# A graph layer on one core: one load of x for two projections, clears and placement steps spread over the first stage, edges loaded four slots ahead

## The chip, the cores and the metric

The kernel runs on one core of a Trainium2 chip. The time is device microseconds of that core for one execution. Five engines run their own instruction streams side by side: PE (matrix multiply), DVE (vector), ACT (scalar and copies), POOL (here: it issues the scatters) and SP (here: it only issues DMAs). Sixteen DMA engines move the data for all of them. An engine takes its instructions strictly in the order in which the program lists them, so an instruction that waits holds back everything behind it on its engine. That holds for SP too: a DMA that waits for a free buffer holds back the DMAs behind it.

## The reference

There are 6,250 nodes with 128 features, and 100,000 edges sorted by `dst`.

```python
row, col = (edge_index[0], edge_index[1])
msg_in = jnp.concatenate([x[row], x[col], edge_attr], axis=-1)
h = msg_in @ W + b
mu = jnp.mean(h, axis=-1, keepdims=True)
var = jnp.mean(jnp.square(h - mu), axis=-1, keepdims=True)
h = (h - mu) * jax.lax.rsqrt(var + LN_EPS) * gamma + beta
msg = jax.nn.relu(h)
out = jax.ops.segment_sum(msg, row, num_segments=x.shape[0])
...
x = _layernorm(x + _L0_gnn_ref(x, edge_index, edge_attr_128, W, b, gamma, beta), axis=-1)
```

`W` has three blocks of 128 rows: for the source node, the target node and the edge. So `h` is a sum of three projections, of `x[src]`, of `x[dst]` and of the edge features.

## The kernel before

**Tiles, slots, stages.** Edges are cut into 782 tiles of 128. Four tiles are a *piece*, and the main loop handles one piece in each *slot* `q`, from 0 to 195. The tiles are divided into five stages (`SPLITS`, L37): slots 0 to 40 are stage 0, then 42 slots, 42, 41 and 30.

**What a slot does.** `edge_loads` (L460) loads the edge features `eT` and the targets' positions `db`, for `DG` = 3 pieces at a time, in two buffers. `edge_window` (L478) loads a window of 42 rows of the projected targets from a table in memory (`xb_d`), in three bf16 parts whose sum has nearly float precision; the table is one of three (`TABLES`), chosen by the slot (`TABLE_FROM`). `edge_hot` (L490, DVE) turns `db` into a one-hot matrix `ohd`, two slots ahead of its use. `edges` (L503, PE) multiplies edge features by `W` (L512) and adds the window's rows through the one-hot (L516). `scatters` (L520) copies the result from PSUM to `hs` (ACT, L524 and L525) and scatters its 128 rows for each tile to a place in `sorted_d` (POOL, L529, four indirect DMAs a slot). `hs` has eight buffers, so the slots may run ahead of the scatters by eight.

**Places.** `places` (L356) works out where each edge's row goes, for a group of 12, 24 or some 42 tiles. It is a generator of eleven steps on DVE and PE: a one-hot over blocks (L368), a running count (L372), counts over partitions (PE, L384 and L385), the offsets (L391, L394), a sum on PE (L409), the place (L413 to L426). Its steps are dealt to slots by hand (`at_slots`, L805 to L810). The *first*, *second* and *third* places are the groups of 12, 24 and 43 tiles at the start of stage 0. `source_blocks` (L228) prepares the block numbers of a range of tiles on DVE.

**Projections in stage 0.** `project(g, k)` (L308) projects four blocks of 128 nodes. With `k` = 1 it makes the target tables: it multiplies `x` by the second block of `W`, splits the result into three bf16 parts on ACT and DVE (L331 to L339) and writes them to the tables (SP, L345). With `k` = 0 it makes `xa`, the sources' projection, which stays in SBUF. Each of the two has its own array of `x` in memory (`xN` in node order, `xT` in block order), loaded by `load_x` (SP, L107) in three buffers. One projection starts in three slots of four and goes on by one step in each slot after.

**Clears.** Before a stage's rows are scattered, the part of `sorted_d` that may stay empty is filled with a marker: `clear_pairs` (L861) issues one DMA (L192) for each of the 25 pairs of blocks of a stage.

**Second half of each stage.** From five slots into the next stage on, `load_pair` (L572, SP, L576) reads the sorted rows of two blocks back (`hl`), and the class `Pair` adds the sources' part, normalizes, applies the relu and sums by node. `work(n)` deals these steps to the slots. The last stage's pairs follow after the last slot, with the final layer norm (`Finish`).

**The order.** PE, DVE, ACT and SP run in the order in which the program lists their work; nothing is reordered. In each slot of stage 0 the list is: projections' next steps, edge loads, the window, clears of the next stage, `edge_hot`, `edges`, `scatters`, places' steps, a new projection with its load of `x`, clears of stage 0, and what `others` names for this slot.

Of the kernel before, what the change touches and what calls it, by code (L numbers as in the profile page):

```python
# [8 lines left out]
F32 = mybir.dt.float32  # L9
# [6 lines left out]
P = 128  # L16
# [10 lines left out]
PT = 4  # L27
WN = 42

TABLES = [(0, 512), (0, 1536), (1024, 6656)]  # L30
PIECES = 196
TABLE_FROM = [0, 13, 40, PIECES]
HALF = PIECES // 2
BANKS = {"hp": 2, "sel": 3, "tr": 1}

# [29 lines left out]
def dram_ap(t, offset, ap):  # L65
    return bass.AP(tensor=t.tensor, offset=t.offset + offset, ap=ap)
# [16 lines left out]
def fast_path(ctx, tc, io, bad_d):  # L83
# [22 lines left out]

    def load_x(g, k):  # L107
        xT = proj_pool.tile([P, XG * P], F32, name="xT", bufs=3)
        n = min(XG * P, (NPAD if k == 0 else TABLES[-1][1]) - g * XG * P)
# [193 lines left out]

    xa = tabs.tile([P, NB, 3 * D], BF16, name="xa")
    acc = tabs.tile([P, NB, ACW], F32, name="acc")
    n_proj = [-(-NB // XG), TABLES[-1][1] // (XG * P)]

    def project(g, k):  # L308

        t0 = g * XG
        m = min(XG, NB - t0) if k == 0 else XG
        xT = xT_of.pop((g, k))
        name = ("sel", "sel", "tr", "sel")[g % 4]
        ps = psum.tile([P, XG, P], F32, name=name, bufs=BANKS[name])
        for j in range(m):
            nc.tensor.matmul(ps[:, j, :], xT[:, j * P:(j + 1) * P], w[:, k, :],
                             start=True, stop=True)
        yield  # L320
        full = ps[:, :m, :]
        if k == 0:
            o = [xa[:, t0:t0 + m, i * D:(i + 1) * D] for i in range(3)]
            full_t = proj_pool.tile([P, XG, D], F32, name="full", bufs=2)
            full = full_t[:, :m, :]
            nc.vector.tensor_tensor(full, ps[:, :m, :], row_bc(bias, m), op=ALU.add)
            yield
        else:
            xb_t = proj_pool.tile([P, 3, XG, D], BF16, name="xb", bufs=4)
            o = [xb_t[:, i, :, :] for i in range(3)]  # L330
        nc.scalar.copy(o[0], full)  # L331
        yield
        rest_t = proj_pool.tile([P, XG, D], F32, name="rest", bufs=2)
        rest = rest_t[:, :m, :]
        nc.vector.tensor_tensor(rest, full, o[0], op=ALU.subtract)
        yield
        nc.scalar.copy(o[1], rest)
        yield
        nc.vector.tensor_tensor(o[2], rest, o[1], op=ALU.subtract)  # L339
        yield  # L340
        if k == 1:
            n0 = g * XG * P
            for (lo, hi), t in zip(TABLES, xb_d):
                if lo <= n0 < hi:
                    nc.sync.dma_start(  # L345
                        dram_ap(t, (n0 - lo) * D, [[XG * D, P], [(hi - lo) * D, 3], [1, XG * D]]),
                        xb_t.rearrange("p i t d -> p i (t d)"))
        yield


# [100 lines left out]
        nc.vector.tensor_copy(bad_d, bad_n)  # L451


    HS, DG = 8, 3
    hs_all = [const.tile([P, PT, ROW], F32, name=f"hs{i}") for i in range(HS)]
    for h in hs_all:
        nc.gpsimd.memset(h[:, :, D:ROW], 0.0)
# [2 lines left out]
    def edge_loads(q, queue=None):  # L460

        if q % DG or q >= PIECES:
            return
        t0 = q * PT
        g = min(DG, PIECES - q)
        eT = edge.tile([P, DG * PT * P], F32, name="eT", bufs=2)
        db = edge.tile([P, DG * PT * P], BF16, name="db", bufs=2)
        for n in ([(0, g)] if q else [(i, 1) for i in range(g)]):
            c0, c1 = n[0] * PT * P, min((n[0] + n[1]) * PT * P, (TILES - t0) * P)
            nc.sync.dma_start(eT[:, c0:c1], io["eT"][:, t0 * P + c0:t0 * P + c1])  # L470
            c1 = (n[0] + n[1]) * PT * P
# [272 lines left out]
    def run(g, n=1):  # L744
        for _ in range(n):
            next(g, None)
# [114 lines left out]
    def clear_pairs(s, n):  # L861
        for p0 in range(cleared[s], min(cleared[s] + n, NB // 2)):
# [3 lines left out]
                tc.add_to_no_dep_group("clear", i.ins)  # L866
            cleared[s] = p0 + 1

    for s, (n_tiles, _, _, _) in enumerate(SPLITS):
        p0, p1 = first_tile[s] // PT, -(-first_tile[s + 1] // PT)  # L870
        slots = p1 - p0
        for i in range(slots):
            q = p0 + i
            for g in groups:
                run(g)
            edge_loads(q + 3)
            edge_window(q + 3)
            if s + 1 < n_split and i >= slots - 30:
                clear_pairs(s + 1, 1 if slots > NB // 2 else 2)
            edge_hot(q + 2)  # L880
            edges(s, q)
            n = steps_due(q + 1) - n_steps
            work(min(n, 1))
            scatters(s, q)
            for g in steps_at.pop(q, []):
                run(g)
            work(n - 1)
            if s == 0:
                if todo and q % 4 != 3:
                    groups = groups[-5:] + [project(*todo.pop(0))]  # L890
                    run(groups[-1])
                    if loads:
                        load_x(*loads.pop(0))
                if 2 <= i:
                    clear_pairs(0, 2)
            if q in others:
                others.pop(q)()
        if s == 0:
            assert not todo and late
# [302 lines left out]
```

## Time and profile before

| | us |
|---|---|
| median of three runs | 1479.99 |
| lowest and highest run | 1478.99, 1490.42 |
| own time of the profiled execution | 1186.86 |
| its span, first to last instruction | 1184.9 |
| PE busy (mean granted clock 0.917 of full) | 969.5 (82%) |
| DVE busy | 926.8 (78%) |
| POOL busy | 837.2 (71%) |
| ACT busy | 623.4 (53%) |
| bytes moved, mean rate | 247.79 MB, 209 GB/s |

The profile is of one execution, and that execution took 293 us less than the median of the runs. Its parts are read against its own time. "Busy" leaves out the time in which an engine waits, and also the time in which it only issues: POOL's scatters count 0.97 us each, and some 0.3 us between two of them is not counted. A line of the timeline gives the start, the duration, the engine, the line of the program, the operation, and in brackets the idle time before it with what ended that. A line of the table of waits gives who waited for whom, the total, how many times, and the longest.

### The profile page before, as it was taken

The page shows a single profiled execution, that of the slowest core. Times are in us where ns is not written, and L with a number is a line of the kernel's source. Part 1 is how long each engine was busy: PE and PEld are TensorE (multiplying, and loading weights), DVE is VectorE, ACT ScalarE, POOL GpSimd, SP SyncE. Part 2 cuts the span into 40 slices and gives each one's busy share as a digit, 9 for nine tenths or more (in the row PEclk, how much of TensorE's full clock was granted, in tenths as well). Part 3 has the DMA queues.
Part 4 walks back from the last instruction along what each step waited for, and adds up shares of the span by engine and source line. Part 5 has one row for each costly group of instructions (what it writes and reads, how often), then busy time and mean ns, then how long its engine had stood idle before and what let it go on. Part 6 is the DMA issues. An engine that isn't in the chain of part 4 may idle for free.

```text
span 1184.9 us, 27181 instructions
## 1 busy us (share of the span) xinstructions
PE 969.5 (82%) x9050; PEld 849.0 (72%) x9050; DVE 926.8 (78%) x2504; ACT 623.4 (53%) x2848; POOL 837.2 (71%) x899
## 2 busy tenths in 40 slices
PE   3565576656889899798989979999898999999994
PEld 2554466545778787687877868788787889877883
DVE  8765288716698997779889778987888788888996
ACT  1222233113465465455556455546555677768996
POOL 2575677777777777777777777777777777743664
PEclk9786687766999999899999989999999999999998
DMA  6499787538587864677877657786766576534551
GB/s 199 151 287 277 233 272 232 182 101 295 170 264 245 262 205 161 221 239 238 264 230 224 193 190 217 250 263 209 227 214 202 183 230 222 170 124 133 161 168 58
DMA packets 113948, 247.79 MB, mean 209 GB/s; under 512 B 45691, under 2 KB 59020, under 8 KB 113798
## 3 DMA queue, kind: packets, MB, share of 16 engines
q1 hardware_dynamic: 87668, 191.99, 52.6%
q0 software_dynamic: 25152, 53.18, 12.7%
q8 instruction: 73, 1.20, 0.4%
q10 hardware_dynamic: 978, 0.80, 0.2%
q14 instruction: 77, 0.63, 0.2%
HBM read 158.36 MB, written 87.52 MB: 208 GB/s over the span
## 4 chain that ended last, share of the span: by engine, by line
DMA 24%; PE 23%; POOL 18%; DVE 14%; issue 10%; ACT 9%; SPq 2%; ACTq 0%; POOLq 0%; DVEq 0%
POOL sorted L529 18%; DMA sorted<-hs,place_i 18%; PE pa L669 6%; DMA db<-drel_d 4%; PE sel L628 4%; PE hp L512 4%; PE beside L409 3%; ACT sq L645 3%; DVE msg L660 3%; PE sel L624 3%; DVE ohe L597 2%; DVE sc L372 2%; ACT ohn L613 2%; ACT fsq L715 2%; PE tr L609 2%
## 5 line engine op out<-in xcount | busy, mean ns | idle before, releaser
L529 POOL DMA_INDIRECT sorted<-hs,place_i x782 | 769.9, 985 | 265.5 <-issue 195.8
L524 ACT COPY hs<-hp 128x512 f32<-128x512 f32 x196 | 114.2, 583 | 390.9 <-DMA sorted<-hs,place_i 234.4
L512 PE MATMUL hp<-w,eT 128*128 128x128 f32 x1564 | 237.8, 300 | 35.1 <-ACT hs L524 26.6
L669 PE MATMUL pa<-msg,ohe 128*128 128x130 f32 x1900 | 246.8, 283 | 13.0 <-DVE acc L677 5.5
L660 DVE SCALAR_TENSOR_TENSOR msg<-sel,rstd,cut 128x128 f32<-128x128 f32 x875 | 247.2, 345 | 9.4 <-PE tr L609 0.5
L628 PEld LDWEIGHTS <-ohn 128*128 128x128 bf16 x2850 | 178.3, 99 | 94.8 <-issue 71.5
L645 ACT ACTIVATE sq<-sel 128x128 f32<-128x128 f32 x875 | 230.4, 282 | 18.1 <-PE sel L628 12.8
L512 PEld LDWEIGHTS hp<-w,eT 128*128 128x128 f32 x1564 | 211.7, 210 | 38.4 <-ACT hs L524 29.0
L669 PEld LDWEIGHTS pa<-msg,ohe 128*128 128x128 f32 x1900 | 228.3, 195 | 15.2 <-issue 8.1
L628 PE MATMUL sel<-xa,ohn 128*128 128x128 bf16 x2625 | 183.6, 222 | 14.8 <-ACT ohn L613 14.0
L645 ACT ACTIVATION_READ_ACCUMULATOR sq<-sel 128x1 f32 x875 | 186.1, 213 | 0.0
L597 DVE TENSOR_TENSOR ohe<-hl,beside 128x1024 f32<-128x1024 f32 (+1 forms) x125 | 144.3, 1156 | 45.8 <-DMA hl<-sorted 19.1
L500 DVE TENSOR_SCALAR ohd<-db,part_w 128x512 bf16<-128x512 bf16 x194 | 71.5, 369 | 93.9 <-DMA db<-drel_d 77.9
L624 PE MATMUL sel<-hl,ident 128*128 128x512 f32 (+1 forms) x250 | 130.6, 605 | 14.2 <-DVE msg L660 14.0
L613 ACT COPY ohn<-tr 128x1024 bf16<-128x1024 bf16 (+1 forms) x125 | 120.6, 965 | 18.3 <-PE tr L609 18.1
L609 PE MATMUL tr<-ident_h,ohe 128*128 128x128 bf16 x950 | 76.2, 224 | 19.7 <-DVE ohe L597 19.7
L516 PE MATMUL hp<-win,ohd 126*128 126x128 bf16 x782 | 81.1, 229 | 9.6 <-DVE ohd L500 5.5
L638 DVE TENSOR_TENSOR sel<-sel,hl 128x512 f32<-128x512 f32 x100 | 69.1, 691 | 12.8 <-PE sel L628 12.8
L648 ACT ACTIVATE std<-ss,eps 128x4 f32<-128x4 f32 (+1 forms) x250 | 74.3, 297 | 8.1
L609 PEld LDWEIGHTS <-ohe 128*128 128x128 bf16 x950 | 60.0, 100 | 22.0 <-DVE ohe L597 21.8
L409 PE MATMUL beside<-far,ident 128*128 128x294 f32 (+10 forms) x304 | 75.3, 402 | 0.0
L516 PEld LDWEIGHTS <-ohd 126*128 126x128 bf16 x782 | 64.5, 103 | 14.3 <-DVE ohd L500 9.0
(156 smaller groups left out, 967.3 us busy)
## 6 DMA issues: line engine op xcount, KB each, us to landing
hl<-sorted SPq DMA_DIRECT2D x100, 528.0 KB
eT<-in_eT SPq DMA_DIRECT2D x64, 768.0 KB
sorted<-empty SPq DMA_DIRECT2D x125, 198.0 KB
db<-drel_d SPq DMA_DIRECT2D x64, 384.0 KB
sorted<-hs,place_i POOLq DMA_INDIRECT x782
hl<-sorted SPq DMA_DIRECT2D x25, 396.0 KB
win<-xb_d SPq DMA_DIRECT2D x196, 31.5 KB
xb_d<-xb SPq DMA_DIRECT2D x15, 384.0 KB
```

The costliest lines, as they stand in the source:

```text
L512: nc.tensor.matmul(hp[:, j, :], eT[:, at], w[:, 2, :], start=j == 0, stop=False, skip_group_check=True)
L516: nc.tensor.matmul(hp[:, j, :], oh[:3 * WN, at], win[:3 * WN, :], start=False, stop=j == m - 1, skip_group_check=True)
L524: evict = nc.scalar.copy(hs[:, :m, 0:D], hp[:, :m, :])
L529: i = nc.gpsimd.indirect_dma_start(out=sorted_d[s][:, :], out_offset=bass.IndirectOffsetOnAxis(ap=place_i[:parts, t:t + 1], axis=0), in_=h ...
L597: nc.vector.tensor_tensor(self.ohe[:, :k, :], self.hl[:, :k, D:D + 1].to_broadcast([P, k, P]), row_bc(iota_p, k), op=ALU.is_equal)
L609: nc.tensor.transpose(tr[:, j, :], half[:, j0 + j, 1::2], ident_h)
L613: nc.scalar.copy(self.ohn[:, :self.k, :], self.tr[:, :self.k, :])
L624: nc.tensor.matmul(sel[:, :m, :], ident, rows, start=True, stop=False)
L628: nc.tensor.matmul(sel[:, j, :], self.ohn[:, j0 + j, :], xa[:, b, i * D:(i + 1) * D], start=not on_pe and i == 0, stop=(j == m - 1 and i = ...
L645: nc.scalar.activation(sq[:, j, :], self.sel[g][:, j, :], AF.Square, accum_out=ss[:, j:j + 1])
L660: nc.vector.scalar_tensor_tensor(self.msg[:, j0 + j, 0:D], self.sel[g][:, j, :], rstd[:, j:j + 1], cut, op0=ALU.mult, op1=ALU.max)
L669: nc.tensor.matmul(self.pa[:, h, :], self.ohe[:, j, :], self.msg[:, j, :], start=(j == h), stop=(j == k - 2 + h))
```

## The change

- **Tables.** The third table covers all 6,400 padded nodes in block order instead of nodes 1,024 to 6,656 in node order, and is used from piece 45 instead of 40. It is written by a new kind of projection, `k` = 2, which reads the same loaded `x` (`xT`) as `k` = 0, right before it. `k` = 1 remains for the first three groups. So 3 loads of `xN` and 13 of `xT` remain of 13 and 13, and 29 projections are made instead of 26. The list of projections alternates `k` = 2 and `k` = 0; a load of `xT` is issued when every second projection starts.
- **Edges.** `DG` is 2 instead of 3, with three buffers instead of two. Loads and windows are issued for slot `q + 4` instead of `q + 3`, after a start of four slots. Pieces 2 and 3 are loaded with piece 0 before the loop.
- **Clears.** Stage 0's clears go from two in each slot from slot 2 on to two and one in turn from slot 1 on. Stage 1's begin 26 slots before the end of stage 0 instead of 30.
- **Places and other steps.** The third places' eleven steps go from slots 3 to 7 to slots 2 to 8. `source_blocks` moves from slots 4 and 8 to 8 and 12, the weights of `k` = 0 and the biases from 6 and 7 to 2 and 3, `open_late` from 40 to 44.

```diff
-TABLES = [(0, 512), (0, 1536), (1024, 6656)]
+TABLES = [(0, 512), (0, 1536), (0, NPAD)]
-TABLE_FROM = [0, 13, 40, PIECES]
+TABLE_FROM = [0, 13, 45, PIECES]
...
-        m = min(XG, NB - t0) if k == 0 else XG
-        xT = xT_of.pop((g, k))
-        name = ("sel", "sel", "tr", "sel")[g % 4]
+        m = XG if k == 1 else min(XG, NB - t0)
+        xT = xT_of[g, k % 2]
+        name = ("sel", "sel", "tr", "sel")[n_banks % 4]
+        n_banks += 1
...
-            nc.tensor.matmul(ps[:, j, :], xT[:, j * P:(j + 1) * P], w[:, k, :],
+            nc.tensor.matmul(ps[:, j, :], xT[:, j * P:(j + 1) * P], w[:, min(k, 1), :],
...
+        if k == 2:
+            nc.sync.dma_start(
+                dram_ap(xb_d[2], t0 * D, [[NB * D, P], [NPAD * D, 3], [1, m * D]]),
+                xb_t[:, :, :m, :].rearrange("p i t d -> p i (t d)"))
...
-    HS, DG = 8, 3
+    HS, DG = 8, 2
...
-        eT = edge.tile([P, DG * PT * P], F32, name="eT", bufs=2)
-        db = edge.tile([P, DG * PT * P], BF16, name="db", bufs=2)
+        eT = edge.tile([P, DG * PT * P], F32, name="eT", bufs=3)
+        db = edge.tile([P, DG * PT * P], BF16, name="db", bufs=3)
...
-            (nc.sync if q else nc.gpsimd).dma_start(
+            (nc.sync if q > 2 else nc.gpsimd).dma_start(
...
     edge_loads(0)
+    edge_loads(2)
     run(first)
...
-    load_x(3, 1)
+    load_x(0, 0)
...
-    todo = [(g, 1) for g in range(1, n_proj[1])] + [(g, 0) for g in range(n_proj[0])]
-    loads = todo[3:]
+    todo = [(g, 1) for g in range(1, n_proj[1])]
+    todo += [(g, k) for g in range(n_proj[0]) for k in (2, 0)]
+    loads = {2 * g + n_proj[1] - 4: (g, 0) for g in range(1, n_proj[0])}
+    n_todo = len(todo)
     others = {1: lambda: bases(range(1, len(TABLES))),
-              4: lambda: source_blocks(8 * n0, TILES // 2),
-              8: lambda: source_blocks(TILES // 2, TILES),
-              6: lambda: weights(0, 1), 7: biases, 10: check_early, 36: check_windows,
-              37: check_bases, 38: cuts, 40: lambda: open_late()}
+              8: lambda: source_blocks(8 * n0, TILES // 2),
+              12: lambda: source_blocks(TILES // 2, TILES),
+              2: lambda: weights(0, 1), 3: biases, 10: check_early, 36: check_windows,
+              37: check_bases, 38: cuts, 44: lambda: open_late()}
...
-            at_slots = [3, 3, 4, 4, 4, 4, 5, 5, 6, 7, 7]
+            at_slots = [2, 2, 3, 3, 3, 5, 5, 6, 6, 7, 8]
...
-            edge_loads(q + 3)
-            edge_window(q + 3)
-            if s + 1 < n_split and i >= slots - 30:
+
+            while ahead <= min(q + 4, 3 + q + q // 3):
+                edge_loads(ahead)
+                edge_window(ahead)
+                ahead += 1
+            if s + 1 < n_split and i >= slots - (30 if s else 26):
...
-                    if loads:
-                        load_x(*loads.pop(0))
-                if 2 <= i:
-                    clear_pairs(0, 2)
+                    if n_todo - len(todo) in loads:
+                        load_x(*loads.pop(n_todo - len(todo)))
+                clear_pairs(0, 1 + i % 2 if 1 <= i else 0)
```

More of the change, by code (lines that the diff above doesn't have):

```diff
@@ L108, in load_x @@
         xT = proj_pool.tile([P, XG * P], F32, name="xT", bufs=3)
-        n = min(XG * P, (NPAD if k == 0 else TABLES[-1][1]) - g * XG * P)
+        n = min(XG * P, (NPAD, TABLES[1][1])[k] - g * XG * P)
         nc.sync.dma_start(xT[:, :n], io[("xT", "xN")[k]][:, g * XG * P:g * XG * P + n])
@@ L305, in fast_path @@
     acc = tabs.tile([P, NB, ACW], F32, name="acc")
-    n_proj = [-(-NB // XG), TABLES[-1][1] // (XG * P)]
+    n_proj = [-(-NB // XG), TABLES[1][1] // (XG * P)]
+    n_banks = 0
     def project(g, k):
+        nonlocal n_banks
         t0 = g * XG
-        m = min(XG, NB - t0) if k == 0 else XG
-        xT = xT_of.pop((g, k))
-        name = ("sel", "sel", "tr", "sel")[g % 4]
+        m = XG if k == 1 else min(XG, NB - t0)
+        xT = xT_of[g, k % 2]
+        name = ("sel", "sel", "tr", "sel")[n_banks % 4]
+        n_banks += 1
         ps = psum.tile([P, XG, P], F32, name=name, bufs=BANKS[name])
         for j in range(m):
-            nc.tensor.matmul(ps[:, j, :], xT[:, j * P:(j + 1) * P], w[:, k, :],
+            nc.tensor.matmul(ps[:, j, :], xT[:, j * P:(j + 1) * P], w[:, min(k, 1), :],
                              start=True, stop=True)
@@ L329, in project @@
             xb_t = proj_pool.tile([P, 3, XG, D], BF16, name="xb", bufs=4)
-            o = [xb_t[:, i, :, :] for i in range(3)]
+            o = [xb_t[:, i, :m, :] for i in range(3)]
         nc.scalar.copy(o[0], full)
@@ L342, in project @@
             n0 = g * XG * P
-            for (lo, hi), t in zip(TABLES, xb_d):
+            for (lo, hi), t in zip(TABLES[:2], xb_d):
                 if lo <= n0 < hi:
@@ L867, in clear_pairs @@
             cleared[s] = p0 + 1
+    ahead = 3
     for s, (n_tiles, _, _, _) in enumerate(SPLITS):
@@ L898, in fast_path @@
         if s == 0:
-            assert not todo and late
+            assert not todo and not loads
     work(4 * len(pairs) + LEAD + 18 - n_steps)
@@ L1178 @@
     xT = xp.reshape(P, NB, D).transpose(2, 1, 0).reshape(D, NB * P)
-    n_all = TABLES[-1][1]
+    n_all = TABLES[1][1]
     xN = np.zeros((n_all, D), x.dtype)
-    xN[:N] = x
+    xN[:] = x[:n_all]
     xN = xN.reshape(n_all // (XG * P), P, XG, D).transpose(3, 0, 2, 1).reshape(D, n_all)
```

## The prediction

> **What bounds the kernel now.** I read the page first, for the engine that repeats. Its first column of the second block below is the group, then busy time and mean ns of one, then the idle time just before them and what ended most of it.
>
> ```profile
> span 1184.9 us, 27181 instructions
> POOL 2575677777777777777777777777777777743664
> DMA  6499787538587864677877657786766576534551
> L529 POOL DMA_INDIRECT sorted<-hs,place_i x782 | 769.9, 985 | 265.5 <-issue 195.8
> L500 DVE TENSOR_SCALAR ohd<-db,part_w 128x512 bf16<-128x512 bf16 x194 | 71.5, 369 | 93.9 <-DMA db<-drel_d 77.9
> ```
>
> POOL stands at 7 tenths from the fifth slice to the thirty-fifth and never moves: that is a metronome, not an engine with slack. The timeline of POOL shows its beat: a scatter takes 0.97 us, and the next follows 0.30 us later, whatever is ready. It is broken in one stretch only:
>
> ```profile
> 49.30 0.97 POOL L529 DMA_INDIRECT sorted<-hs,place_i  x1 [0.31 <-issue]
> 58.58 0.97 POOL L529 DMA_INDIRECT sorted<-hs,place_i  x1 [8.31 <-ACT hs L525]
> ...
> 94.97 0.97 POOL L529 DMA_INDIRECT sorted<-hs,place_i  x1 [3.89 <-ACT hs L525]
> ...
> 133.26 0.96 POOL L529 DMA_INDIRECT sorted<-hs,place_i  x1 [0.31 <-issue]
> 140.45 0.97 POOL L529 DMA_INDIRECT sorted<-hs,place_i  x1 [6.23 <-ACT hs L525]
> ```
>
> The sum: first scatter at 23.9, 782 x 1.27 = 993, gaps for hs, long scatters (782 x (985 - 967 median) = 14), last one ended at 1053.9, then 131.0 of last-stage pairs and output. 23.9 + 993 + 23.4 + 14 + 131 = 1185, the span; the execution's own time is 1186.86. What is the 23.4? The table of waits, taken for 23 to 142 us alone (total, times, longest):
>
> ```profile
> ACT xb L331 <- DMA xb_d<-xb: 37.5, 7, 11.6
> DVE ohd L500 <- DMA db<-drel_d: 33.4, 5, 9.6
> PE beside L384 <- DVE cnt L381: 27.0, 3, 13.8
> POOL sorted L529 <- ACT hs L525: 23.4, 6, 8.3
> ```
>
> POOL's six waits for hs are 23.4 us (27.4 in the whole span). The chain of waits for the first 170 us (start, us, what) names what stands behind the first of them, and the stretches of 30 us (DMA share and GB/s last) why it was late:
>
> ```profile
> 40.02 7.95 DMA db<-drel_d
> 48.06 0.35 DVE ohd L500
> 48.41 2.31 DVE sc L372
> 50.75 2.45 DVE sc L372
> ...
> 60.00:90.00 30.00, 18.22 (x122) 15.44 (x121) 18.06 (x45) 7.53 (x18) 22.16 (x22) 0.85 0.94 292
> 90.00:120.00 30.00, 15.62 (x97) 14.76 (x97) 15.98 (x27) 8.52 (x21) 17.98 (x19) 0.61 0.91 274
> ```
>
> DVE stands in order: while it waits for db at 48, the 43-tile places step behind it waits, PE waits for its counts (13.8 us at 53.7), behind that the edge matmuls, then hs, then POOL. DMA is full: per slot a first-stage program moves 256 KB eT, 128 db, 31.5 win, 264 scatter, 2 clears x 198, 3/4 x 256 xT, 3/4 x 384 xb: 1,555 KB, which at the mean of the two rows' last column, 283 GB/s, is 5.6 us, over the 5.08 of four scatters.
>
> At the other end the chain reads:
>
> ```profile
> 831.21 7.02 DMA sorted<-hs,place_i
> 838.37 0.59 ACT hs L524
> ```
>
> From there to the end it runs over PE, DVE and ACT, but it hangs on a scatter through the hs buffers (8 slots), so a POOL that is earlier moves all of it.
>
> **The change part by part.** *One load of x, two projections.* 10 of 13 xN loads go (10 x 256 KB = 2.6 MB), 13 xT loads stay. Table 2 is written in 13 pieces (12.5 x 384 KB) instead of 11: +0.6 MB. Net -2.0 MB, 7 us of DMA time at 283 GB/s. Projections go from 26 to 29: each added one is eight rows of PE (1.1 us when warm, 2.05 cold), two ACT copies (0.59 + 0.62) and two DVE subtracts (0.69 + 0.68): +3.3 PE, +3.6 ACT, +4.1 DVE us, spread to slot 36 where POOL's lead covers them (DVE is 4.8 us busy of 30 at 240 to 270). They end four slots later, and table 2 is first read at slot 41, two slots after its last write (entry 26 of the list starts in slot 34, its write is five slots on): 10 us, against the 1.1 to 11.6 us that ACT waited for such writes; if it is late, up to 8 slots x 5.08 us of POOL's filled hs stand before it. Nothing charged. The xT load now takes a buffer freed one projection before, so SP no longer stands at L110 for the matmul just issued (22.4 + 9.0 us between 23 and 260, with db and win loads queued behind).
>
> *Clears spread.* 1.5 a slot instead of 2, stage 1's from slot 15, not 11. No bytes go. Per slot now: 256 + 128 + 31.5 + 264 + 297 + 96 (xT) + 144 (xb) = 1,217 KB, 4.4 us at 283 GB/s, under the beat. In slots 15 to 17 both clears meet: 2.5 x 198, 1,415 KB, 5.1 us: even, for three slots. The last clear is issued at slot 17; scatters from slot 19 wait for it. A landing of 8 us (like db's) fits in two slots; without that cover, one wait of 8 us at most.
>
> *Third places spread.* Same instructions; PE's count matmul comes two slots after DVE's cnt instead of in the same slot, so edge matmuls no longer stand behind it. DVE's need in slots 2 to 8: places 13.6 (oh 2.45, scans 4.8, cnt and at 1.1, far 2.5, product 1.3, rest 1.5), source blocks 3.8 (53.6 to 57.4), weights and biases 1.6, ohd 7 x 0.35, 5.5 projections x 1.7: 31 us of 35.6. It fits, narrowly. What can remain is between 0 and 9.9 (the two gaps there, 8.3 and 1.6, unchanged); the near row is the 1.55 us at 70 us, where DVE was full and not waiting. I take 4 with the even slots 15 to 17.
>
> *Edges two pieces at a time, four slots ahead.* 98 loads of eT and db instead of 65: 66 more DMAs on SP at a median of 0.36 and 0.42 us, 26 us of a queue whose five longest waits sum to 509. db is asked for at slot q for ohd of slot q + 2, not q + 1: 10 us against landings of 7 to 9. That takes most of DVE's 77.9 us; after 142 POOL never starved, so there it is worth nothing but perhaps 1 us at the end (db wait at 1002 us in the chain; POOL's last landing is only some 5 us ahead of the final pairs' start). At the start, 256 KB more of eT go ahead of the first windows: 1.2 us at the 226 GB/s of 20 to 30 us, of which 0.3 is covered (the first hs was done at 23.59, the scatter began at 23.88): +1. The bounds are 0, as eT of piece 0 still goes first, and 1.2.
>
> Here a rule speaks against the change. The trace has db landings of 7.95 and 8.87 us for 384 KB behind 768. The Trainium skill ("DMA: Bandwidth & Descriptors", Measured under Bandwidth, and the fit in Anatomy of one DMA) wants 1 MiB a transfer, and gives a fixed 2.0 us to each. By it 66 more transfers are 132 us of transfer latency, and if POOL stood behind each, the kernel would be 113 us slower. The same trace has 16 engines 0.94 busy with five kinds of transfer overlapped, so the fixed part runs beside other transfers: I take 0, and the rule's fit was made on another queue kind.
>
> Sum: 23.4 - 4 residual - 1 start + 1 end = 19.4 us off 1186.86: 1167.5.
>
> **The runs shown** lie 293 us above that execution (1478.99 to 1490.42), and the profile doesn't say where. If it is POOL's beat (293/782 = 0.37 us a scatter), a slot is 6.6 us, the 5.6 us of DMA fit before the change too, and perhaps 8 us are left to gain. If it is DMA (247.79 MB in 1480 is 167 GB/s), 2.0 MB are 12 us, and the gaps are larger than seen. If it is PE or lies outside, all 19.4 stay. I carry the difference over as it is: 1479.99 - 19.4 = 1460.6.
>
> **The rivals.** *Hidden* (0.28): the beat of the runs is slower or DVE's 31 of 35.6 us don't fit; 0 to 14 us gained, 1466 to 1480. For it: the 293 us. Against: gaps of 6.2 us at 140 are DMA's, not DVE's.
> *Slower* (0.16): SP in its order. An edge load waits for the matmuls of the slot before (L470, 82.4 us in 38 waits, 2.2 each); 33 more such holds are 72 us, and pair loads (L576) stand behind them. From 840 us PE and DVE have no slack, so a hold that makes hl late is paid. hl is asked for six steps ahead, 1.5 slots at the last stretch's four steps a slot; it decides when holds eat those 8 us. A quarter of 72 exposed is 18 us, nearly cancelling the gain; half is 36: 1480 + 36 - 19 = 1497. Against: DVE waited for hl four times, 19.1 us in all.
> *Not done* : if db is asked for earlier but SP still stands at L110 or L470, the first gap stays and 10 us are gained: inside the second case.
>
> **How the numbers follow.** Gaps closed: 0.56, own range 1447 (all 23.4 and 3 at the end, by 1.25) to 1465. A measurement of this kernel tells about 1%, 14.8 us. Faster by more than that (under 1465.2) 0.56, within 0.29, slower 0.15. The range reaches 1440 (DMA-short runs with larger gaps) to 1486, leaving out 2 in 10, mostly of the slower case.
>
> **What would show it.** POOL's waits for hs before 142 us near 4, not 23.4; last scatter ends near 1035; DVE's waits for db under 25 us; DMA share at 60 to 120 below 0.9; SP's waits at L110 nearly gone. Wrong if POOL shows new gaps at slots 17 to 19 or 41, if hl waits grow after 840, or if POOL closes its gaps and the runs don't follow.

## The result: 0.3% faster where 1.3% was forecast

| | before | after |
|---|---|---|
| median of 20 runs each, us | 1472.69 | 1469.45 |
| lowest to highest, us | 1464.44 to 1490.42 | 1464.94 to 1486.12 |

The ratio is 0.9972, with a 95% interval of 0.9949 to 0.9995: some 3 to 4 us of 1473 where 19.4 were forecast. The time lies in the range of the prediction, which was 46 us wide, and the direction is right, but the gain is about a sixth to a fifth of what the sum gave. Even that is small beside what lies between sessions: the medians of the kernel before in three later ones of the same kind are 1478 to 1490 us.

One thing has to be known to read the rest: the runs of this kernel fall in two conditions, of 1167 to 1192 us and of 1461 to 1507 us for the kernels before and after, and in each of the five sessions of the experiments (each on another chip) all runs were in the same one. They are called A and B here. The profile that the prediction was worked out from was an execution in A; the runs it was to predict were in B, and so is the profile of the changed kernel. On which chips those were taken is not on record.

The page of the changed kernel first: its span, PE's and POOL's tenths in 40 slices, the shares of the chain that ended last, and the two groups that answer to those shown of before.

```profile
span 1468.7 us, 27422 instructions
PE   4736455446877878786868778787877998888995
POOL 3667666665555555555655555555555554550565
PE 55%; issue 16%; DVE 12%; another core or an unknown queue 8%; ACT 7%; DMA 1%; SPq 1%; ACTq 0%; DVEq 0%
L536 POOL DMA_INDIRECT sorted<-hs,place_i x782 | 770.9, 986 | 532.3 <-ACT hs L532 310.6
L507 DVE TENSOR_SCALAR ohd<-db,part_w 128x512 bf16<-128x512 bf16 x194 | 69.5, 359 | 66.4 <-remote 53.1
```

POOL's scatters take what they took before (986 ns against 985), but POOL's row of sevens has become a row of fives, while PE's stands at 7 to 9 in the second half: the beat of 1.27 us is gone. Before, the scatters' idle time was mostly their own issue time (195.8 of 265.5 us); now 310.6 of 532.3 us are waits for `hs`. POOL is starved all along and has no share in the chain, which runs over PE and over time in which an engine waits for nothing that the trace names ("issue"). The table of waits of the same execution (total, times, longest) has both:

```profile
POOL sorted L536 <- ACT hs L532: 310.6, 110, 6.7
...
PE sel L635 <- issue: 71.2, 104, 2.3
...
PE hp L519 <- issue: 67.5, 46, 12.9
...
PE tr L616 <- issue: 46.6, 62, 1.4
```

Summed over all of PE's lines, these gaps without a releaser (over 0.15 us each) are 260.5 us, in 307 gaps. In the profile of before there are none. PE's timeline from 611 to 616 us shows what they look like (start, duration, line, count, and in brackets the gap):

```profile
610.81 0.77 PE L635 MATMUL sel<-xa,ohn 128*128 128x128 bf16 x11
612.42 0.26 PE L635 MATMUL sel<-xa,ohn 128*128 128x128 bf16 x1 [0.83 <-issue]
612.48 0.31 PE L616 MATMUL tr<-ident_h,ohe 128*128 128x128 bf16 x1
613.85 0.37 PE L616 MATMUL tr<-ident_h,ohe 128*128 128x128 bf16 x2 [1.06 <-issue]
614.55 0.29 PE L616 MATMUL tr<-ident_h,ohe 128*128 128x128 bf16 x1 [0.33 <-issue]
615.25 0.61 PE L616 MATMUL tr<-ident_h,ohe 128*128 128x128 bf16 x4 [0.41 <-issue]
```

Within eight transposes (L616) PE stops three times, for 1.06, 0.33 and 0.41 us, and waits for nothing that the trace shows. In the program, neither these matmuls nor the weight loads before them wait for a semaphore.

Not every gap is of this kind. The traces in B hold fewer than half as many semaphore records as those in A (for the kernel before, 10,867 and 24,940), so a wait whose end was not recorded shows as "issue" too, or as "remote" and "another core or an unknown queue" in a program of one core. Counted over the instructions, 46 of the 307 gaps, with 73.8 of the 260.5 us, stand before a matmul that does wait for a semaphore. The longest, 12.9 us in the row of `hp`, is one of them and waits for ACT. The other 261 gaps, with 186.7 us, stand before a matmul that waits for none.

### The profile page after: what moved, and what is told of

Same layout as the page of the kernel before. It is cut to its first block, busy times and chain, and to the rows that moved or that the text cites. A ratio compares the mean times of both kernels' runs of the same rounds, so it can differ in the third digit from the quotient of the medians.

```text
span 1468.7 us, 27422 instructions
## 1 busy us (share of the span) xinstructions
PE 1084.8 (74%) x9070; PEld 923.6 (63%) x9070; DVE 934.8 (64%) x2510; ACT 625.9 (43%) x2854; POOL 838.4 (57%) x899
## 4 chain that ended last, share of the span: by engine, by line
PE 55%; issue 16%; DVE 12%; another core or an unknown queue 8%; ACT 7%; DMA 1%; SPq 1%; ACTq 0%; DVEq 0%
PE pa L676 15%; PE hp L519 11%; PE sel L635 9%; PE beside L416 6%; PE sel L631 6%; PE tr L616 4%; PE hp L523 3%; ACT sq L652 2%; DVE ohe L604 2%; DVE sc L379 2%; DVE msg L667 1%; ACT ohn L620 1%; ACT fsq L722 1%; PE sel L321 1%
## 5 line engine op out<-in xcount | busy, mean ns | idle before, releaser
L536 POOL DMA_INDIRECT sorted<-hs,place_i x782 | 770.9, 986 | 532.3 <-ACT hs L532 310.6
L652 ACT ACTIVATE sq<-sel 128x128 f32<-128x128 f32 x875 | 231.0, 283 | 211.9 <-remote 159.3
L519 PE MATMUL hp<-w,eT 128*128 128x128 f32 x1564 | 252.4, 306 | 86.0 <-issue 67.5
L676 PE MATMUL pa<-msg,ohe 128*128 128x130 f32 x1900 | 296.0, 315 | 24.6 <-issue 20.8
L676 PEld LDWEIGHTS pa<-msg,ohe 128*128 128x128 f32 x1900 | 273.3, 225 | 28.7 <-issue 23.7
L635 PEld LDWEIGHTS <-ohn 128*128 128x128 bf16 x2850 | 182.3, 99 | 166.2 <-issue 155.7
L519 PEld LDWEIGHTS hp<-w,eT 128*128 128x128 f32 x1564 | 221.4, 214 | 94.1 <-issue 74.2
L635 PE MATMUL sel<-xa,ohn 128*128 128x128 bf16 x2625 | 203.8, 223 | 74.3 <-issue 71.2
L616 PE MATMUL tr<-ident_h,ohe 128*128 128x128 bf16 x950 | 93.0, 237 | 57.9 <-issue 46.6
L523 PE MATMUL hp<-win,ohd 126*128 126x128 bf16 x782 | 89.9, 233 | 37.1 <-issue 33.8
L616 PEld LDWEIGHTS <-ohe 128*128 128x128 bf16 x950 | 67.2, 106 | 72.0 <-issue 57.8
L416 PE MATMUL beside<-far,ident 128*128 128x294 f32 (+10 forms) x304 | 80.7, 420 | 2.5 <-issue 2.4
```

Of the source, the lines that this page charges most:

```text
L416: nc.tensor.matmul(sums[:, :g * T], wt, flat(v[:, b:b + g, :]), start=(k == 0 and b == 0), stop=(k == 1 and b + PG >= NB), skip_group_chec ...
L519: nc.tensor.matmul(hp[:, j, :], eT[:, at], w[:, 2, :], start=j == 0, stop=False, skip_group_check=True)
L523: nc.tensor.matmul(hp[:, j, :], oh[:3 * WN, at], win[:3 * WN, :], start=False, stop=j == m - 1, skip_group_check=True)
L536: i = nc.gpsimd.indirect_dma_start(out=sorted_d[s][:, :], out_offset=bass.IndirectOffsetOnAxis(ap=place_i[:parts, t:t + 1], axis=0), in_=h ...
L616: nc.tensor.transpose(tr[:, j, :], half[:, j0 + j, 1::2], ident_h)
L635: nc.tensor.matmul(sel[:, j, :], self.ohn[:, j0 + j, :], xa[:, b, i * D:(i + 1) * D], start=not on_pe and i == 0, stop=(j == m - 1 and i = ...
```

## The experiments

### Who paces the kernel in the runs (B)

Theory at this point: in the runs another engine than POOL sets the pace, most likely PE with its gaps. The rival: POOL's own path is slower there. Four kernels, beside a median of 1490.34 us for the kernel before.

The kernel before again, for its profile in this condition:

> The kernel before, unchanged, to have its trace in the same condition as its twenty runs (1464 to 1490 us); the one profile of it that the prediction rests on took 1187. Theory PE: the runs' 290 us are gaps in PE's own stream for which the trace names no releaser (0 in that profile, 262 us in the profile of the changed kernel). Expected: time 1465 to 1490, over 200 us of such gaps on PE, clock near 0.85, POOL's waits for hs over 250 us, and the last first-stage scatter at about the same time as in the changed kernel. Rival POOL: the beat of the scatters is slower in the runs; expected then 1.6 us from scatter to scatter and few waits for hs. If the time is again near 1187, the kernel has two conditions and the comparison has to be made in each.

Measured: 1500.52 us in its one execution. From its table of waits:

```profile
POOL sorted L529 <- ACT hs L525: 341.4, 114, 7.1
...
PE sel L628 <- issue: 82.2, 118, 1.8
```

PE's gaps are 270.8 us in all, 318 of them, and the granted clock 0.837 against 0.917 in A. So they are not the change's doing. POOL's scatters take 986 ns here too, which speaks against the rival. Before 142 us POOL waited 22.8 us for `hs` (the changed kernel: 13.3), but after that it waits another 319 us, where in A it waits 4.

POOL loaded with more work (on top of the changed kernel):

```diff
+            nc.gpsimd.memset(idle_t, 0.0)
+            nc.gpsimd.memset(idle_t, 1.0)
```

> The changed kernel with two small memsets on POOL after every scatter, which give POOL some 0.2 to 0.4 us more per scatter, 782 times: 160 to 310 us more of POOL work. Theory PE: POOL idles 310 us waiting for hs in the runs, so most of it is hidden: the time rises by 0 to 50 us. Rival POOL (its beat sets the pace): the time rises by all of it, 160 us or more.

Measured: 1722.66 us in one execution, some 240 more than the changed kernel would take beside that median (1486 us, by its ratio of 0.9972). POOL's timeline says why this tells nothing:

```profile
604.75 0.97 POOL L537 DMA_INDIRECT sorted<-hs,place_i  x1 [0.30 <-issue]
605.70 0.21 POOL L542 MEMSET idle_t<- 128x100 f32 x1
605.97 0.18 POOL L543 MEMSET idle_t<- 128x100 f32 x1
...
615.57 0.98 POOL L537 DMA_INDIRECT sorted<-hs,place_i  x1 [0.53 <-issue]
```

The memsets didn't stay behind their scatters; they came in bunches, 38 in a row here, and the next scatter stood ten us behind them. So the statement that an engine takes its instructions strictly as the program lists them doesn't hold for POOL in this trace; what moved them isn't shown. The price is that of another order, and the experiment is inconclusive.

Less work for PE (the changed kernel with the third bf16 part of `xa` left out, so the product has less precision):

```diff
-                for i in range(3):
+                for i in range(2):
...
-                                     stop=(j == m - 1 and i == 2) if on_pe else i == 2)
+                                     stop=(j == m - 1 and i == 1) if on_pe else i == 1)
```

> The changed kernel with two of the three bf16 parts of the sources' projection multiplied in pick: the third part is left out, so 950 of 2850 weight loads and matmuls of that line go. Theory PE: 24 of these take 1.34 us when they run freely, so 53 us of PE's work go, and some tenth of the 262 us of gaps: the time falls by 60 to 90 us. Rival POOL or DMA: nothing that they do is touched; the time falls by 0 to 15 us.

Measured: 1462.91 us (one execution), 0.982 of the kernel before. Beside the same 1486 us of the changed kernel, 950 matmuls less of 9070 bring about 23 us, but single executions of the kernel before, run beside it, spread over 29 us. It lies between the theories and suggests that PE's work counts. PE's busy time fell by 21.7 us (1084.8 to 1063.1), where 53 were expected, and its gaps were 237.2 us.

Of the change, only the edge loads (two pieces a load, three buffers, four slots ahead):

```diff
-    HS, DG = 8, 3
+    HS, DG = 8, 2
...
+    edge_loads(2)
...
-            edge_loads(q + 3)
-            edge_window(q + 3)
+            while ahead <= min(q + 4, 3 + q + q // 3):
+                edge_loads(ahead)
+                edge_window(ahead)
+                ahead += 1
```

> The kernel before with one part of the change: edges loaded two pieces at a time in three buffers, four slots ahead. As predicted from the 1187 us profile it would take away most of DVE's waits for db and give some 12 us. Theory PE: DVE's waits for db are behind PE's own gaps in most slots; the time moves by less than 6 us either way. Rival (the queue of SP: 66 more transfers hold the pair loads): slower by 10 us or more.

Measured: 1.0006 (0.9981 to 1.003): worth nothing in B.

### The pair where the prediction's profile was taken (A)

The next session was in condition A, beside a median of 1187.56 us for the kernel before. What was expected of its runs had been written for B.

> The kernel before once more, for a trace from the same chip and the same minutes as the next run (changed kernel), so that slots can be compared one by one. Expected from the first such pair, which came from two sessions: the scatters of slot 40 begin 5 to 9 us later here than in the changed kernel, and what is left of that at slots 100 and 166 and at the end tells where it goes. Theory PE (PE's stream with its gaps is the bound after slot 40): the lead stays whole, 5 to 9 us at the end. Rival (another engine or transfer takes over later): the lead shrinks from slot to slot.

> The changed kernel again, beside the kernel before on one chip. The recorded ratio is 0.9972. Theory PE: 0.993 to 0.997 (5 to 9 us of first stage kept). Rival: 0.997 to 1.001.

Before: 1187.79. After: 1167.27, a ratio of 0.9834 (0.9819 to 0.985), 20.3 us; the prediction's sum was 19.4. The page of the changed kernel in A:

```profile
span 1164.8 us, 27422 instructions
POOL 2777777777777777777777777777777777734664
PE 23%; DMA 23%; POOL 18%; DVE 13%; ACT 10%; issue 10%; SPq 0%; ACTq 0%; POOLq 0%; DVEq 0%
L536 POOL DMA_INDIRECT sorted<-hs,place_i x782 | 769.3, 984 | 246.0 <-issue 194.2
L507 DVE TENSOR_SCALAR ohd<-db,part_w 128x512 bf16<-128x512 bf16 x194 | 72.7, 375 | 43.1 <-DMA db<-drel_d 22.0
```

The slices two to five, 5, 7, 5 and 6 in the profile of before, are all 7: the beat, which held there from the sixth slice on (not the fifth, as the prediction has it), now holds from the second. The waits from 23 to 142 us, first of before, then of after:

```profile
DVE ohd L500 <- DMA db<-drel_d: 32.8, 6, 9.8
...
POOL sorted L529 <- ACT hs L525: 21.3, 9, 9.1
```

```profile
DVE ohd L507 <- DMA db<-drel_d: 13.2, 6, 4.8
...
POOL sorted L536 <- ACT hs L532: 2.9, 5, 1.4
```

18.4 us of POOL's gaps are gone there. What is won there is kept: slot 40's scatters begin 18.6 us earlier than in the kernel before, slot 100's 18.7, slot 166's 20.0, and the last scatter ends at 1033.5 instead of 1053.1 us.

In the same session, 24 matmuls with no use, placed ahead of slot 30's edges in the kernel before: if POOL sets the pace they should vanish, if PE does they should arrive.

```diff
+            if q == 30:
+                idle = psum.tile([P, 512], F32, name="pa")
+                for _ in range(24):
+                    nc.tensor.matmul(idle, ident, flat(empty)[:, 0:512], start=True, stop=True)
```

> The kernel before with 24 matmuls of 128x512 f32 added on PE in slot 30, some 20 us by the 0.86 us that two rows of such a matmul take in the trace, with no waits of their own. Theory PE: PE leads the scatters by only 3 to 10 us in the runs, so 12 to 20 us of it arrive at the end: ratio 1.008 to 1.014. Rival (first stage hidden under POOL's beat, as the 1187 us profile has it, where PE leads by 27 us at slot 32): under 4 us, ratio under 1.003.

PE's timeline has them at 182 us, with 20.82 us:

```profile
182.15 20.82 PE L885 MATMUL pa<-empty,ident 128*128 128x512 f32 x48
```

Measured: 0.9995 (0.9982 to 1.0008). All 20.8 us vanish, within 1 us or so.

And the changed kernel with more of the sums of the second half taken from PE and given to DVE:

```diff
-BY_DVE = [(0,), (0,), (0,), (0,), ()]
+BY_DVE = [(0, 1), (0, 1), (0, 1), (0, 1), ()]
```

> The changed kernel with BY_DVE naming both groups of a pair in the first four stages, so that the sorted rows are added by DVE (0.69 us a group) instead of by an identity matmul on PE: 100 matmuls of two rows each leave PE (0.86 us each, 86 us), 69 us come to DVE, which is 62% busy in the runs. Theory PE: faster by 40 to 90 us, near 1390 to 1430. Rival POOL: no change. Rival DVE: slower by up to 69 us.

Measured: 0.9816 (0.9798 to 0.9835), which overlaps the changed kernel's own interval (0.9819 to 0.985): the work of PE that was taken away isn't what counts in A. PE's busy time fell by 61 us there (969.0 to 907.7), not by 86.

### The same questions in B

Beside a median of 1478.14 us, with the two kernels of before and the edge loads both ways.

> The kernel before with only the edge part of the change (two pieces at a time, three buffers, four slots ahead). Two conditions have shown: in one the kernel takes 1187 us and PE has no gap without a releaser, in the other 1470 to 1500 us and PE has 220 to 270 us of such gaps. In the first, theory Beat (POOL's scatters set the pace, each gap that POOL loses in the first stage is kept to the end): the db waits behind the gaps at 50 and 140 us get shorter, but DMA stays full with clears and x loads: 3 to 10 us of the 20 are gained, ratio 0.992 to 0.997. Rival Lead (the lookahead is the whole gain): 0.983 to 0.987. In the second condition: 1.000 again, as measured (1.0006).

> The changed kernel with the edge part undone (three pieces at a time, two buffers, three slots ahead): what tables, clears, places and moved steps do without it. In the 1187 us condition, theory Beat: most of the gain is here, as DMA is no longer full: 10 to 17 us, ratio 0.986 to 0.992. Rival Lead: under 4 us, ratio over 0.997. In the other condition: 0.995 to 1.000.

> The kernel before with some 20 us of matmuls added on PE in slot 30, again. In the 1187 us condition it was hidden (0.9995). In the other condition, theory PE (PE with its gaps is the bound there from the first stage on): 12 to 20 us arrive at the end, ratio 1.008 to 1.014. Rival (slack elsewhere, as before): under 1.003.

> The changed kernel with the sorted rows of both groups added by DVE instead of PE, again: 86 us of PE's matmuls go, 69 us come to DVE. In the 1187 us condition nothing beyond the change itself (0.9816 was measured, 0.9834 for the change). In the other condition, theory PE: faster by 40 to 90 us, ratio 0.94 to 0.97. Rival (waits between engines, not PE's amount of work, make up the loss): within 10 us of the changed kernel, ratio 0.990 to 1.004.

The matmuls of slot 30 take the same time on PE here:

```profile
202.02 20.82 PE L885 MATMUL pa<-empty,ident 128*128 128x512 f32 x48
```

but now they cost: 1.01 (1.0058 to 1.0143), 14.8 us (8.6 to 21.1) for 20.8. The same kernel in A cost nothing. This pair shows, for slot 30, where the slack is: in A a delay of PE is hidden, in B most or all of it arrives at the end.

The edge loads alone gave 1.0006 (0.9983 to 1.003), as in the other B session; the change without them 0.9938 (0.9913 to 0.9963).

DVE's additions gave 0.9997 (0.9972 to 1.0022), no gain for 200 matmuls less on PE; the rival was right. In its one profile PE works 50 us less than in the changed kernel's (1034.6, 1084.8) and idles 59 us more. The group of ACT's squares, first in the changed kernel, then in this one, shows that nothing moved up:

```profile
L652 ACT ACTIVATE sq<-sel 128x128 f32<-128x128 f32 x875 | 231.0, 283 | 211.9 <-remote 159.3
```

```profile
L652 ACT ACTIVATE sq<-sel 128x128 f32<-128x128 f32 x875 | 230.4, 282 | 209.3 <-DVE sel L645 191.7
```

ACT idles before its squares as long as it did (209.3 us, 211.9 in the changed kernel, where the trace puts most of it to no engine it can name). What ends the idle time is now mostly DVE's addition. That fits the rival, waits between engines, but doesn't single out one. So PE's amount of work in the second half isn't the bound in B.

### The parts alone in A

Beside a median of 1187.02 us. The clears alone, and the third places alone (with the moved `source_blocks`, weights and biases):

```diff
-            if s + 1 < n_split and i >= slots - 30:
+            if s + 1 < n_split and i >= slots - (30 if s else 26):
...
-                if 2 <= i:
-                    clear_pairs(0, 2)
+                clear_pairs(0, 1 + i % 2 if 1 <= i else 0)
```

```diff
-            at_slots = [3, 3, 4, 4, 4, 4, 5, 5, 6, 7, 7]
+            at_slots = [2, 2, 3, 3, 3, 5, 5, 6, 6, 7, 8]
```

> The kernel before with only the edge part. In the 1187 us condition, theory Beat: 3 to 10 us of the 20 (ratio 0.992 to 0.997), as DMA stays full; rival Lead: nearly all (0.983 to 0.987). In the 1470 us condition: 1.000 a third time (1.0006 and 1.0006).

> The changed kernel with the edge part undone. In the 1187 us condition, theory Beat: 10 to 17 us (0.986 to 0.992); rival Lead: under 4 us. In the 1470 us condition: 0.994 again, or, if that was chance, 0.997 like the whole change.

> The kernel before with only the clears spread (one and two a slot from slot 1 on; the next stage's from 26 slots before the end). In the 1187 us condition: the DMA queue is full from 60 to 140 us with 1,555 KB a slot; 99 KB a slot less leave it 5.3 us a slot, still over POOL's 5.08, so 1 to 6 us are gained (0.995 to 0.999). Rival (clears are the whole excess): 10 us or more. In the 1470 us condition: 0.997 to 1.001.

> The kernel before with only the third places' steps, source blocks, weights and biases moved. In the 1187 us condition: PE no longer waits 13.8 us at 53.7 for the counts of the same slot, but the wait of DVE for db at 48 stays, so the gap of 8.3 us shrinks to 2 to 5 us: 3 to 6 us gained (0.995 to 0.9975). Rival (DVE was late because of db alone): nothing. In the 1470 us condition: 0.997 to 1.002.

| kernel in A | us | ratio to before | POOL's waits for `hs` between the first scatter and 142 us |
|---|---|---|---|
| edge loads alone | 1180.81 | 0.9943 (0.992 to 0.9965) | 10.6 |
| clears alone | 1177.71 | 0.9914 (0.989 to 0.9937) | 13.0 |
| places alone | 1179.06 | 0.993 (0.9906 to 0.9954) | 13.8 |
| all but the edge loads | 1167.87 | 0.9824 (0.9798 to 0.9851) | 4.7 |
| all | 1167.27 (session before) | 0.9834 (0.9819 to 0.985) | 2.9 |

The clears brought 9.3 us and the places 8.0, both more than was expected of them; the edge loads' ratio is in the range that theory Beat gave. Everything but the edge loads brings the whole gain, within the intervals (19.2 us by the medians, 20.3 with them), and more than was expected of it. POOL's timeline shows which gap each one leaves: of the clears alone, then of the places alone.

```profile
57.88 0.97 POOL L529 DMA_INDIRECT sorted<-hs,place_i  x1 [7.24 <-ACT hs L525]
...
92.07 0.97 POOL L529 DMA_INDIRECT sorted<-hs,place_i  x1 [3.29 <-ACT hs L525]
```

```profile
51.39 0.97 POOL L529 DMA_INDIRECT sorted<-hs,place_i  x1 [1.49 <-ACT hs L525]
...
131.56 0.97 POOL L529 DMA_INDIRECT sorted<-hs,place_i  x1 [5.96 <-ACT hs L525]
```

In the kernel before, in this condition, the gaps are 9.09 us at 60, 4.32 at 97, 1.32 at 115 and a last one of 3.6 at 140. The places take the first one down to 1.49 but leave a longer last one; the clears shorten the first less, and all but take away the last (0.91 is left). The two cure different gaps. With the edge loads alone 5.02, 1.81 and 3.77 us are left, and where the other parts are in place they find little more to take (4.7 us without them, 2.9 with them). The tables alone, and clears with places, weren't run in A: how the 19.2 us without the edge loads split between clears, places and tables is known only from the two parts alone, 9.3 and 8.0.

### The parts alone in B

Beside a median of 1479.29 us: clears with places, and the tables (one load of `x` for two projections, as in the diff of the change) alone.

> The kernel before with the clears spread and the third places' and other steps moved, and neither the single load of x nor the edge part. In the 1187 us condition: places take the gap at 60 us (9.1 to 1.5), clears shrink those from 97 to 140 us (10.6 to 4.2 in the trace with clears alone), different gaps, so their gains of 9.3 and 8.0 us add: 13 to 17 us, ratio 0.986 to 0.989. Rival (each gap closed shows another one behind it): no more than the larger of the two, ratio over 0.991. In the 1470 us condition: 0.995 to 1.000.

> The kernel before with only the single load of x for both projections (with the weights and biases at slots 2 and 3 that it needs, and the tables' limits). In the 1187 us condition: half of xT's and more than half of the tables' writes leave slots 2 to 14, 400 KB of 1,555 a slot, so DMA is no longer full from 90 to 140 us and 5 to 10 us of the gaps there go; the one at 60 us stays: ratio 0.991 to 0.996. Rival (clears alone are the excess): under 3 us. In the 1470 us condition: 0.995 to 1.000.

Measured: 0.9941 (0.9913 to 0.9969) and 0.9935 (0.9903 to 0.9967). With the 0.9938 without the edge loads, both groups of parts and their sum lie at the same 0.6% in B, a little more than was expected, and they don't add. Nothing in these profiles names which wait it is that each of them ends: single executions in B differ by over a per cent, more than is looked for.

## Why the prediction failed in its size

**The step that failed** is the carrying over: "If it is PE or lies outside, all 19.4 stay. I carry the difference over as it is". The runs are this case, most of the added time is in PE's own row, and the 19.4 do not stay: 20.3 us in A became 3 to 4 in B. The prediction saw that the runs lay 293 us above its profile and treated them as the same schedule with something added. They are another schedule. The first line of the page of the kernel before, in A and then in B, has PE's share of it:

```profile
PE 967.0 (82%) x9050; PEld 848.1 (72%) x9050; DVE 927.6 (78%) x2504; ACT 622.6 (52%) x2848; POOL 838.8 (71%) x899
```

```profile
PE 1100.2 (73%) x9050; PEld 936.7 (63%) x9050; DVE 933.0 (62%) x2504; ACT 623.6 (42%) x2848; POOL 838.3 (56%) x899
```

The span grew by 313 us (1185.9 to 1498.6). The same matmuls keep PE busy 133 us longer, at a mean granted clock of 0.837 instead of 0.922, PE stops for 271 us without a releaser, and its other idle time is 91 us less. DVE, ACT and POOL are as busy as before. So PE falls behind POOL's beat, and POOL waits for `hs` 110 times over the whole span. A gap of POOL at 58 us is then one of many waits for an engine that is late anyway. By my reckoning over the traces, a slot's last edge matmul ends 42 us ahead of its first scatter at slot 40 in A, before and after, and 33 and 34 us at slot 166: POOL works off a queue that is filled ahead of it. In B it is 8 us before and 12 after at slot 40, 5 and 6 at slot 100, and 1 at slot 166. The unused matmuls of slot 30, free in A and 14.8 us in B, show it without a trace, for that slot. In the later slots, giving 200 of PE's matmuls to DVE brought nothing (0.9997). That points to a chain of waits there, in which PE and its stops have the largest share, rather than to PE's amount of work; its links were not tested one by one.

The sentence before it, that a slower beat of POOL would leave "perhaps 8 us", and the case called *Hidden* had the size right, but for POOL's beat or DVE's load; neither was the reason (a scatter takes 986 ns in B, and DVE is 62% busy).

**The sum**, on its own ground, was right in its total: 19.4 us forecast, 20.3 measured in A. Its terms:

- *Gaps of POOL before 142 us, 23.4 to a residual of 4*: 21.3 to 2.9 in the pair of A. Right, the residual a little large. Each of the six waits in the 23.4 us holds the 0.30 us that the beat of 1.27 counts already, so the sum has 1.8 us twice.
- *Start, +1*: the first scatter began at 24.62 before and 24.70 after. The 256 KB ahead of it cost 0.1 us, since that scatter waits for a step of DVE (`src_f`) in both. With the edge loads alone it begins at 25.38 and waits for `hs`. But in the two profiles of the kernel before it begins at 23.88 and at 24.62, so no cost under 1 us can be read here.
- *End, -1*: from the last scatter to the end, 132.8 before and 131.4 after. The size is right, but the other profile of the kernel before has 131.0, so this shows no gain.
- *Last scatter near 1035*: 1033.5. *DVE's waits for `db` under 25 us*: 22.0. *SP's waits at L110 nearly gone*: 32.4 us for the projections' matmuls before, 1.1 after. All three right.
- *DMA share at 60 to 120 us below 0.9*: wrong. The stretches of 30 us (PE, PEld, DVE, ACT and POOL busy, clock, DMA share, GB/s) in A, before and after:

```profile
60.00:90.00 30.00, 18.46 (x131) 16.03 (x130) 18.25 (x43) 7.42 (x18) 22.82 (x22) 0.89 0.89 274
90.00:120.00 30.00, 15.88 (x97) 14.79 (x98) 17.29 (x28) 7.32 (x18) 18.83 (x20) 0.60 0.94 289
```

```profile
60.00:90.00 30.00, 15.78 (x121) 14.61 (x120) 26.34 (x61) 8.43 (x20) 22.98 (x24) 0.77 0.93 280
90.00:120.00 30.00, 25.99 (x195) 24.48 (x195) 19.45 (x37) 12.64 (x31) 23.30 (x23) 0.84 0.92 269
```

The engines of the DMA are as full as before, though the page has 2.0 MB less moved, as forecast. The stretch does more of the kernel: 45 scatters instead of 40 for 16.5 MB instead of 16.9, and PE works 41.8 us of the 60 instead of 34.3, DVE 45.8 instead of 35.5. So the share of the window stayed while the bytes for one scatter fell; the waits behind it were the thing to name.

**Which part does it.** The prediction didn't split the 23.4 us by part, but it credited the earlier request for `db` with "most of DVE's 77.9 us" and put DVE's wait for `db` at the head of the first gap. In A the change without that part gains as much (0.9824), with the waits for `db` from 23 to 142 us at 15.7 us against 32.8 before. Nor do those waits tell what a part is worth: with the edge loads alone they fall to 19.0 us, for a gain of 6.2 (1187.02 to 1180.81), while with the clears alone they stay at 30.5 and with the places alone at 32.4, for 9.3 and 8.0. The first gap, 9.09 us, fell to 1.49 by the places alone: the places' steps in the order of DVE and PE stood behind it more than the wait for `db`.

**The rule on larger transfers**, weighed there and put at nothing, stays at nothing: with the 66 more, smaller loads the ratio in A is 0.9834, without them 0.9824, and with them alone 0.9943; in B with them alone it is 1.0006. The 113 us that the rule would have made do not show in either condition.

**The rivals.** *Slower (SP in its order)*: SP's holds for edge buffers grew from 91.1 us in 38 waits to 130.7 in 61, so the mechanism is there, but DVE's waits for `hl` only went from 16.4 to 20.7 us, and the time fell by 20.3: in A it reaches the end by a few us at most. *Not done* fell: the SP queue no longer stands at L110.

**Open.** What makes PE's gaps isn't shown. Whether they go with the amount of work isn't either: a tenth fewer matmuls had 237.2 us of them instead of 260.5, but those of the kernels with 9,050 or 9,070 matmuls are anywhere from 219 to 271. In part they go with places in PE's program: of the 271 gaps of the kernel before that stand before a matmul without a wait, 97 recur in the kernel with the slot-30 matmuls within two matmuls of the same place, once the 48 added rows are taken out, where shifts by 20 to 300 matmuls give 5 to 27. Most last about 0.45 or 1.1 us. They don't fall on the transfers of the queues that the page calls "instruction": 12 of the 271 overlap one of 16 KB, and 20 to 27 do when those are shifted by 3 or 6 us. Nor is it shown what makes a session A or B; as its traces also hold fewer records, a part of the recording in it can't be ruled out. Also open is whether the edge loads take something back in B: the intervals with them (0.9949 to 0.9995) and without (0.9913 to 0.9963) come from different sessions and overlap.

**A better version.** The change without its edge loads is the one to keep: 0.9824 in A and 0.9938 in B, with the whole change at 0.9834 and 0.9972. It isn't shown to be faster than the whole change; it does as much with 66 fewer transfers and the simpler loop.

## What to carry to other kernels

Before working a sum from a profile, ask whether that execution is one of the runs: here a quarter of the time between them meant another pace-setter, and closing the gaps of the engine that set the pace in the one was worth little in the other. A block of useless work placed on one engine at one place, run in both, answered that for its place better than any share of busy time. And when several edits close one stretch of gaps, run them alone: here three of four did the whole work in A, and the edge loads, worth 6.2 us alone, added nothing to them.

## What the hardware showed

- The same program takes 1187 us on two chips and 1478 to 1490 on three others (medians of the kernel before), with a mean granted clock of 0.91 to 0.92 and of 0.84 to 0.86 in its runs. Whether the chip or the time decides can't be told, as each session was on another chip.
- In the slower condition PE stops some 300 times, for 0.85 us on average (270.8 us in 318 gaps of the kernel before), with no releaser in the trace; 271 of these gaps, with 190.7 us, stand before a matmul that waits for no semaphore. In the faster condition no such gap is over 0.1 us.
- A scatter of 128 rows has a steady period of 1.27 us (0.97 and 0.30 between) in both conditions, wherever POOL isn't made to wait; it was POOL's supply that differed, not POOL.
